# A sandwich block on one core: the repeated part and the last five blocks of a hand-ordered kernel in a new order

## The chip, the cores and the metric

The kernel runs on one core of a Trainium2 chip. The metric is the device time of one execution in microseconds (us); the runs of a kernel are given by their median. A profile is one more execution, recorded with the start and the length of every instruction; its span runs from the first instruction to the last.

PE is the matmul engine, DVE, ACT and POOL are the three engines for elementwise work, SP issues the transfers (DMA). Each engine works off its own list in order; between engines, semaphores hold an instruction until what it needs is there.

## What is computed

Four batches of 2048 rows of 256 numbers. Per batch, an attention step and a feed-forward step, each of them between two norms and added to its input:

```python
x = x + layernorm(attn(layernorm(x)))
x = x + layernorm(ffn(layernorm(x)))

def attn(x):
    q, k, v = split(x @ weight_qkv, 3)        # parts of the contraction in fp16
    s = softmax((q / sqrt(256)) @ k.T)
    return (s @ v) @ out_w.T + out_b

def ffn(x):
    x_prev = x shifted by one row, zeros in front
    r = sigmoid((mu_r * x + (1 - mu_r) * x_prev) @ W_r.T)
    k = (mu_k * x + (1 - mu_k) * x_prev) @ W_k.T
    return r * (square(relu(k)) @ W_v.T)
```

## The kernel before

**Blocks.** The rows are cut into 32 blocks of 256 (eight to a batch). A block is a tile of 128 partitions x 2 halves x 256 numbers. The query and key weights are folded into one matrix G, the value and output weights into w_o. Numbers for a matmul are split into a high and a low fp16 tile (`H` and `L` in a name), and a product is then two or three fp16 matmuls.

**The order is written out.** `HEAD`, `LOOP` and `TAIL` are strings of words; `run` calls the function of each word in turn, and every engine's list is the order in which its words stand. `HEAD` prepares weights and the first blocks, `LOOP` is run for block numbers 3 to 26, `TAIL` holds what is left of the last blocks. In `LOOP`, `sM@0` is the current block and `yy@-5` the block five before; in `TAIL`, `@T1` is the last block (31), `@T5` is block 27. What follows a slash chooses a half, or an engine for each half.

**The words that matter here**, by stage:

- Attention. `aS`, `aP`, `aN`, `aM`, `aD`: statistics, power (POOL), norm and split of the input, for a block nine later. `tM` (PE), `tH` (ACT), `tL` (DVE): the block's queries times G. `sM@g/i/h` (PE, 20 matmuls for two): scores of rows half i against half h of the keys, in a buffer of PSUM; there are two such buffers. `sX` (DVE): their maximum; `sB` (DVE): both maxima made into the bias; `sE` (ACT): exponential, which reads the buffer for the last time; `sH` (ACT) and `sL` (DVE): split; `sT` (SP): transpose by DMA into the tile PT. `pv` (PE, 80 matmuls): PT times values, z. `zH`, `zL`: split of z; `pj` (PE): times w_o; `dn` and `y` (DVE): division by the softmax sum, bias.
- Norms after it. `bS` (DVE) statistics, `bP` (POOL) power, `bN` norm, `bA` add to x; the same with c for the second norm, into `hN` and `hF`. Or, in the last blocks: sums on the way of `y` (`q`), `bM` mean (POOL), `bQ` squares (ACT), `bR` power (POOL). The last block has `bY` and `bX` (DVE): subtract the mean, then scale and add in one step.
- Feed-forward. `hX`, `hT`, `hO`: the normed rows transposed by DMA; `hV`, `hW` by PE and a copy instead in the last three blocks; `hC`, `hD` the difference to the row before; `mk`, `mr` the two mixes (DVE; `mA` and `mB` on ACT and POOL instead); `kH`, `kL`, `rH`, `rL` their splits; `kM`, `kR`, `kA` (PE, ACT, DVE): square of relu; `uH`, `uL` its split; `rM`, `rT` (PE, ACT): the gate; `oM` (PE) and `yy` (DVE): its product. Then the same norm forms with d (`dS`, `dP`, `dN`, `dA`; `dM`, `dQ`, `dR`; `dY`, `dX`), and `st` (SP) the store. `ld` loads a block of x again.
- Of the last block alone: `zC` (ACT, L741) copies z unsplit, and `pf`, `kf`, `rf`, `of` are projections in fp32 with weights put together by `wR`.

In the profile most matmuls stand under L173 (a helper) and those of `pv` under L442; the maximum is L396, the exponential L409, the first split L416 and L422, the norms L271 (ACT) and L273 (DVE and POOL), power L213 and L237, squares L227, an add of d L723, `dX` and `bX` L247, `hQ` L542.

Of the kernel before, what the change touches and what calls it, by code (L numbers as in the profile page):

```python
# [64 lines left out]
yy@T10 zH@T7 tM@T4 tH@T4 tL@T4 sM@T5/0/1 sM@T5/0/0 zL@T7 pj@T7 kM@T9 tM@T3 dn@T7 hF@T8/act/pool
sX@T5/0/1 sX@T5/0/0 hN@T8/pool/pool sB@T5/0 y@T7 dS@T10 dn@T6 hX@T8/pool sE@T5/0/0 sE@T5/0/1
sH@T5/0/1 sM@T5/1/0 sX@T5/1/0 sH@T5/0/0 sL@T5/0/0 hT@T8 tH@T3 sM@T5/1/1 hC@T8 sL@T5/0/1 sX@T5/1/1
pv@T6/0/8 sB@T5/1 sM@T4/0/0 sT@T5/0/0 hO@T8/pool hD@T8/dve tL@T3 bS@T7 rM@T9 sE@T5/1/0 kR@T9
sM@T4/0/1 bP@T7 sE@T5/1/1 mr@T8 sH@T5/1/0 sX@T4/0/0 bN@T7/act/pool kA@T9 uH@T9/dve sT@T5/0/1
pv@T6/8/16 sL@T5/1/0 sM@T4/1/1 sH@T5/1/1 mk@T8 sX@T4/0/1 rT@T9 sB@T4/0 sL@T5/1/1 rH@T8/dve bA@T7/dve  # L70
sE@T4/0/1 uL@T9/dve cS@T7 zH@T6 kH@T8/dve sM@T4/1/0 cP@T7 sT@T5/1/1 dP@T10 kL@T8/pool zL@T6
sE@T4/0/0 sX@T4/1/1 sH@T4/0/1 sX@T4/1/0 pj@T6 hC@T7 y@T6 sL@T4/0/1 kM@T8 sB@T4/1 bS@T6
dN@T10/act/pool sT@T5/1/0 kR@T8 sH@T4/0/0 kA@T8 oM@T9 hF@T7/pool/pool hN@T7/act/act bP@T6 sT@T4/0/1
hX@T7/pool yy@T9 pv@T5/0/8 dS@T9 sE@T4/1/1 sM@T3/0/1 hT@T7 hO@T7/pool bN@T6/dve/act sE@T4/1/0
rL@T8/dve bA@T6/dve tM@T2 sH@T4/1/1 sL@T4/0/0 hD@T7/pool tH@T2 cS@T6 sX@T3/0/1 tL@T2 mk@T7 sH@T4/1/0
sL@T4/1/1 kH@T7/act sM@T3/0/0 pv@T5/8/16 cP@T6 hF@T6/act/dve hN@T6/act/act rM@T8 sT@T4/0/0 kL@T7/dve
hX@T6/pool sX@T3/0/0 hC@T6 wR/w_v/dve dn@T5 zH@T5 uH@T8/act sB@T3/0 zL@T5 hT@T6 uL@T8/dve sT@T4/1/1
kM@T7 pj@T5 rT@T8 sE@T3/0/0 dP@T9 sL@T4/1/0 mr@T7 y@T5 hO@T6/dve sE@T3/0/1 bS@T5 dN@T9/dve/pool
rH@T7/dve sM@T3/1/0 kR@T7 hC@T5 dA@T10/dve ld@T5 rL@T7/dve hD@T6/pool oM@T8 sT@T4/1/0 sM@T3/1/1
sX@T3/1/0 bP@T5 pv@T4/0/8 pv@T4/8/16 bN@T5/act/act sH@T3/0/0 wR/w_k/pool sM@T2/0/1 sX@T3/1/1  # L80
bA@T5/pool sL@T3/0/0 sH@T3/0/1 cS@T5 sT@T3/0/0 yy@T8 sB@T3/1 mk@T6 kA@T7 cP@T5 sM@T2/0/0 sE@T3/1/1
sL@T3/0/1 rM@T7 uH@T7/act sH@T3/1/1 sE@T3/1/0 zH@T4 uL@T7/dve sL@T3/1/1 sH@T3/1/0 hN@T5/dve/pool
hF@T5/act/act sT@T3/0/1 mr@T6 dS@T8 hX@T5/pool sX@T2/0/1 kH@T6/act zL@T4 sX@T2/0/0 st@T10 rT@T7
dP@T8 kL@T6/pool oM@T7 kM@T6 sM@T2/1/0 sB@T2/0 dA@T9/dve hT@T5 sE@T2/0/1 sL@T3/1/0 yy@T7 sE@T2/0/0
rH@T6/act dn@T4 sH@T2/0/1 hO@T5/dve rL@T6/pool dS@T7 sH@T2/0/0 pj@T4 y@T4 hD@T5/pool sM@T2/1/1 ld@T4
st@T9 sT@T3/1/1 dP@T7 tM@T1 sL@T2/0/1 kR@T6 bS@T4 mr@T5 sT@T3/1/0 pv@T3/0/8 tH@T1 bP@T4 sX@T2/1/1
sX@T2/1/0 kA@T6 sB@T2/1 pv@T3/8/16 sL@T2/0/0 tL@T1 dN@T7/act/pool bN@T4/pool/act sE@T2/1/0
dA@T7/pool sH@T2/1/0 sM@T1/0/0 mk@T5 kH@T5/pool bA@T4/dve cS@T4 dn@T3 sE@T2/1/1 sT@T2/0/0 sM@T1/0/1
kL@T5/pool sT@T2/0/1 rM@T6 cP@T4 kM@T5 zH@T3 hN@T4/act/dve sH@T2/1/1 zL@T3 sL@T2/1/0 hF@T4/act/act
ld@T1 sL@T2/1/1 rT@T6 sX@T1/0/0 sX@T1/0/1 hX@T4/pool rH@T5/pool sB@T1/0 uH@T6/pool sE@T1/0/1  # L90
sT@T2/1/0 pj@T3 kR@T5 sH@T1/0/1 uL@T6/pool rL@T5/pool sE@T1/0/0 dN@T8/act/pool y@T3/01/q sM@T1/1/1
bM@T3 hT@T4 hC@T4 wR/w_o/dve oM@T6 kA@T5 sM@T1/1/0 sT@T2/1/1 st@T7 dn@T2 sH@T1/0/0 sX@T1/1/1 yy@T6
rM@T5 hO@T4/pool bQ@T3 hD@T4/dve bR@T3 pv@T2/0/8 ld@T3 sL@T1/0/0 mk@T4 sX@T1/1/0 sB@T1/1
bN@T3/act/pool pv@T2/8/16 sT@T1/0/0 kH@T4/pool dA@T8/dve bA@T3/dve sE@T1/1/0 sL@T1/0/1 sT@T1/0/1
# [877 lines left out]
```

## Time and profile before

| what | us |
|---|---|
| median of three runs | 799.85 (798.22 to 801.39) |
| the profiled execution | 798.83 |
| its span | 797.0 |
| PE busy in the span | 781.7 |
| PE busy in 100 to 200, 200 to 300, 300 to 400 | 99.71, 100.00, 100.00 |
| PE busy in 720 to 740, 740 to 760 | 20.00, 19.93 |
| DVE busy in 650 to 700, 720 to 740, 740 to 760 | 47.58, 17.85, 19.66 |
| ACT and POOL busy in 650 to 700 | 29.01, 20.34 |

The granted clock of PE was 0.997 over the span. A line of a timeline gives start, length, engine, line, operation, what is written and read, the shape, and in brackets how long the engine had been idle and which instruction ended that. A block of the repeated part takes 23.7 us. The first matmul of the last five blocks' part starts at 638.86, the last of `pv` ends at 768.52.

### The profile page before, as it was taken

The page shows a single profiled execution, that of the slowest core. Times are in us where ns is not written, and L with a number is a line of the kernel's source. Part 1 is how long each engine was busy: PE and PEld are TensorE (multiplying, and loading weights), DVE is VectorE, ACT ScalarE, POOL GpSimd, SP SyncE. Part 2 cuts the span into 40 slices and gives each one's busy share as a digit, 9 for nine tenths or more (in the row PEclk, how much of TensorE's full clock was granted, in tenths as well). Part 3 has the DMA queues.
Part 4 walks back from the last instruction along what each step waited for, and adds up shares of the span by engine and source line. Part 5 has one row for each costly group of instructions (what it writes and reads, how often), then busy time and mean ns, then how long its engine had stood idle before and what let it go on. Part 6 is the DMA issues. An engine that isn't in the chain of part 4 may idle for free.

```text
span 797.0 us, 15916 instructions
## 1 busy us (share of the span) xinstructions
PE 781.7 (98%) x5803; PEld 574.3 (72%) x5803; DVE 696.9 (87%) x1606; ACT 536.3 (67%) x889; POOL 464.6 (58%) x632
## 2 busy tenths in 40 slices
...
GB/s 238 178 146 172 148 153 145 139 133 143 155 141 134 154 119 143 155 157 119 168 117 140 145 169 124 139 118 128 143 123 120 119 119 61 139 122 130 144 71 66
DMA packets 351199, 109.18 MB, mean 137 GB/s; under 512 B 324624, under 2 KB 351120, under 8 KB 351120
## 3 DMA queue, kind: packets, MB, share of 16 engines
...
q14 instruction: 34, 0.28, 0.1%
q10 hardware_dynamic: 272, 0.26, 0.1%
...
## 4 chain that ended last, share of the span: by engine, by line
PE 90%; DVE 5%; DMA 1%; ACT 1%; issue 1%; POOL 0%; POOLq 0%; SPq 0%; ACTq 0%; DVEq 0%
PE z L442 33%; PE s L173 33%; DMA PT__995<-hl__1240 1%; DMA xa__110<-in_x_dram 1%; PE warm__211 L806 0%; PE op__11019 L173 0%; PE warm__520 L806 0%; PE k__11262 L173 0%; DVE x__10522 L247 0%; DVE sm L818 0%; PE o__11191 L173 0%; PE op__10541 L173 0%; DVE mxmx__10570 L396 0%; DVE pstsA__150 L254 0%; PE r__10479 L173 0%
## 5 line engine op out<-in xcount | busy, mean ns | idle before, releaser
L173 PEld LDWEIGHTS <-w_kH 128*128 128x128 f16 x248 | 24.3, 98 | 8.2 <-issue 0.5
L173 PEld LDWEIGHTS <-GH 128*128 128x128 f16 x192 | 18.8, 98 | 3.7 <-DVE tL__334 L372 0.7
L442 PEld LDWEIGHTS <-X__271 128*128 128x128 f16 x160 | 15.7, 98 | 2.2
L442 PEld LDWEIGHTS <-X__6669 128*128 128x128 f16 x160 | 15.7, 98 | 2.2
L442 PEld LDWEIGHTS <-X__5273 128*128 128x128 f16 x160 | 15.6, 98 | 2.2
L442 PEld LDWEIGHTS <-X__189 128*128 128x128 f16 x160 | 15.5, 98 | 2.3 <-issue 0.5
L442 PEld LDWEIGHTS <-X__233 128*128 128x128 f16 x160 | 15.7, 98 | 1.8
L442 PEld LDWEIGHTS <-X__718 128*128 128x128 f16 x160 | 15.7, 98 | 1.8
L442 PEld LDWEIGHTS <-X__324 128*128 128x128 f16 x160 | 15.7, 98 | 1.8
L442 PEld LDWEIGHTS <-X__4575 128*128 128x128 f16 x160 | 15.7, 98 | 1.8
L442 PEld LDWEIGHTS <-X__571 128*128 128x128 f16 x160 | 15.7, 98 | 1.8
L442 PEld LDWEIGHTS <-X__1783 128*128 128x128 f16 x160 | 15.7, 98 | 1.8
L442 PEld LDWEIGHTS <-X__3179 128*128 128x128 f16 x160 | 15.7, 98 | 1.8
L442 PEld LDWEIGHTS <-X__7367 128*128 128x128 f16 x160 | 15.7, 98 | 1.8
L442 PEld LDWEIGHTS <-X__3877 128*128 128x128 f16 x160 | 15.7, 98 | 1.8
L442 PEld LDWEIGHTS <-X__1141 128*128 128x128 f16 x160 | 15.7, 98 | 1.8
L442 PEld LDWEIGHTS <-X__2481 128*128 128x128 f16 x160 | 15.7, 98 | 1.8
L442 PEld LDWEIGHTS <-X__5971 128*128 128x128 f16 x160 | 15.6, 98 | 1.8
L173 PEld LDWEIGHTS <-GL 128*128 128x128 f16 x128 | 12.5, 98 | 3.4 <-issue 0.9
L173 PEld LDWEIGHTS <-w_kL 128*128 128x128 f16 x124 | 12.1, 98 | 1.4
L329 POOL TENSOR_TENSOR X__718<-xa__485,X__718 128x256 f16<-128x256 f32 x1 | 1.7, 1657 | 16.4 <-ACT xa__485 L271 16.4
L273 POOL TENSOR_SCALAR xa__344<-xa__344,rsrna__455,nmrna__456 128x128 f32<-128x128 f32 x2 | 0.9, 449 | 17.2 <-ACT X__571 L271 17.2
...
## 6 DMA issues: line engine op xcount, KB each, us to landing
...
```

The source lines that it names most:

```text
L173: nc.tensor.matmul(out_ap, l, r, start=(i == 0), stop=(i == len(pairs) - 1))
L273: eng(e).tensor_scalar(dst, src, rs[:, j:j + 1], nm[:, j:j + 1], ALU.mult, ALU.add)
L329: eng(e).tensor_tensor(Xh[:, :, 2, :], T["xa", g][:, :, P:D], Xh[:, :, 1, :], ALU.subtract)
L442: nc.tensor.matmul(z[:, int(c), 0:QB], a, p, start=(kt == 0 and n == 0), stop=(kt == KT - 1 and n == len(prs) - 1))
```

## The change

`LOOP` and `TAIL` are new strings; all words do what they did. `HEAD` stays. One function (`aL`) gets an argument for halves that no word uses.

In `LOOP` the same words stand in another order, but for `aN@9`, which moves from POOL to DVE. On PE the two first score halves change places and `sM@0/1/0` stands ahead of `tM@1`; on DVE `tL@1` stands ahead of `sX@0/1/0` and `sX@0/1/1`; on POOL `bA@-2` stands ahead of `aM@9`.

In `TAIL` the order is new on every engine, and some fifty elementwise steps are on another engine (norms, splits, differences, adds). Three things change in form: `zC@T1` and the second part of `pv@T1` are cut in two by the halves of z; block 30's last norm uses statistics on DVE (`yy@T2`, `dS@T2`, `dP@T2`) in place of sums, squares on ACT and `dR`; and in the last block the half j=1 goes first after `of`.

The diff, with `LOOP` whole and of `TAIL` the rows that the prediction speaks of:

```diff
 LOOP = """
-sM@0/0/0 yy@-5 sM@0/0/1 aS@9 zH@-2 dS@-5 hF@-3/act/act zL@-2 dP@-5 sX@0/0/1 kM@-4 pj@-2 dn@-2
-pv@-1/0/8 sX@0/0/0 sB@0/0 hN@-3/act/act y@-2 tM@1 aP@9 sM@0/1/0 dN@-5/act/act sM@0/1/1 aN@9/pool
-hX@-3/pool kR@-4 dA@-5/pool aT@8 bS@-2 hC@-3 kA@-4 sE@0/0/0 sE@0/0/1 bP@-2 sH@0/0/0 sH@0/0/1 hT@-3
-sL@0/0/0 bN@-2/act/act rM@-4 hO@-3/dve sL@0/0/1 tH@1 aL@11 pv@-1/8/16 hD@-3/pool ld@0 sT@0/0/1
-aM@9/pool uH@-4 sX@0/1/0 sX@0/1/1 rT@-4 bA@-2/pool sB@0/1 sE@0/1/0 mk@-3 kH@-3 sH@0/1/0 cS@-2
-uL@-4/pool sE@0/1/1 oM@-4 sH@0/1/1 tL@1 sL@0/1/0 sT@0/0/0 mr@-3 sL@0/1/1 st@-5 kL@-3/pool sT@0/1/0
-rH@-3 rL@-3/pool sT@0/1/1 aD@9/pool cP@-2
+sM@0/0/1 sM@0/0/0 yy@-5 aS@9 zH@-2 hF@-3/act/act dS@-5 zL@-2 dP@-5 sX@0/0/1 kM@-4 pj@-2 dn@-2
+pv@-1/0/8 sX@0/0/0 sM@0/1/0 hN@-3/act/act sB@0/0 y@-2 tM@1 aP@9 dN@-5/act/act sM@0/1/1 aN@9/dve
+hX@-3/pool kR@-4 sE@0/0/0 aT@8 bS@-2 hC@-3 kA@-4 dA@-5/pool sE@0/0/1 bP@-2 sH@0/0/0 sH@0/0/1 hT@-3
+sL@0/0/0 rM@-4 hO@-3/dve sL@0/0/1 bN@-2/act/act tH@1 aL@11 pv@-1/8/16 tL@1 hD@-3/pool ld@0 sT@0/0/1
+uH@-4 sX@0/1/0 sX@0/1/1 rT@-4 bA@-2/pool sB@0/1 sE@0/1/0 mk@-3 kH@-3 sH@0/1/0 cS@-2 aM@9/pool
+uL@-4/pool sE@0/1/1 oM@-4 sH@0/1/1 sL@0/1/0 sT@0/0/0 mr@-3 sL@0/1/1 st@-5 kL@-3/pool sT@0/1/0 rH@-3
+rL@-3/pool sT@0/1/1 aD@9/pool cP@-2
 """
 TAIL = """
...
-bQ@T2 mB@T3/r/pool mA@T3/k kR@T4 kA@T4 bR@T2 bN@T2/act/pool bA@T2/dve rH@T3/act dQ@T5 cS@T2
-sT@T1/1/1 dN@T6/dve/pool mB@T3/k/pool kH@T3/dve uH@T4/pool pv@T1/8/16 uL@T4/dve cP@T2 rL@T3/dve
-zC@T1 dR@T5 hN@T2/act/act pf@T1/1 dn@T1 dA@T6/dve pf@T1/0 y@T1/0 hV@T2 y@T1/1 hC@T2 bS@T1/0/q
-dN@T5/act/pool bS@T1/1/q kL@T3/pool hW@T2/act hD@T2/pool rM@T4 rT@T4 st@T6 bY@T1/0 mA@T2/r mk@T2
-bP@T1/0/q kH@T2/act bX@T1/0 bP@T1/1/q oM@T4 kM@T3 bY@T1/1 rM@T3 hC@T1 kL@T2/pool yy@T4/01/q dM@T4
-kM@T2 kR@T3 dQ@T4 cS@T1/0/q bX@T1/1 kA@T3 cS@T1/1/q cP@T1/0/q uH@T3/act hQ@T1/0 rT@T3 mB@T2/r/pool
-cP@T1/1/q hV@T1/0 uL@T3/dve hQ@T1/1 kR@T2 hV@T1/1 dA@T5/dve rH@T2/act hW@T1/act oM@T3 kA@T2
-rL@T2/dve dR@T4 uH@T2/act dN@T4/act/act yy@T3/01/q hD@T1/pool uL@T2/dve mk@T1 dA@T4/dve rM@T2 st@T5
-oM@T2 rT@T2 dM@T3 mr@T1 kf@T1 yy@T2/01/q rf@T1 dQ@T3 dM@T2 dR@T3 st@T4 kR@T1 dQ@T2 kA@T1 of@T1/1
-rT@T1 of@T1/0 dN@T3/dve/dve dR@T2 dA@T3/dve yy@T1/0 yy@T1/1 dS@T1/0/q dN@T2/pool/act dY@T1/0
-dS@T1/1/q st@T3 dA@T2/pool dP@T1/0/q st@T2 dX@T1/0 st@T1/0 dY@T1/1 dP@T1/1/q dX@T1/1 st@T1/1
...
+sE@T5/1/1 hD@T8/dve sE@T5/1/0 cS@T7 cP@T7 mr@T8 pv@T6/8/16 hC@T7 sH@T5/1/0 sM@T4/1/1 sX@T4/0/0
+sL@T5/1/0 tL@T3 sX@T4/0/1 uL@T9/pool dn@T5 sT@T5/0/1 sH@T5/1/1 sB@T4/0 sE@T4/0/0 sL@T5/1/1 sE@T4/0/1
+mk@T8 rH@T8/dve sX@T4/1/1 zH@T6 hN@T7/act/act sT@T5/1/0 rM@T9 sM@T4/1/0 oM@T9 sH@T4/0/1 zL@T6 rT@T9
...
+sM@T3/1/1 kR@T7 sL@T3/0/0 sX@T3/1/1 bP@T5 wR/w_o/dve hX@T6/pool kA@T7 oM@T8 bN@T5/pool/act sX@T3/1/0
+sB@T3/1 sL@T3/0/1 sT@T4/0/1 bA@T5/pool sT@T4/0/0 sE@T3/1/0 pv@T4/0/8 sM@T2/0/0 dA@T9/dve uH@T7/act
...
+hO@T6/pool hD@T6/dve zH@T4 oM@T7 zL@T4 mk@T6 hX@T5/dve pj@T4 hT@T5 sX@T2/0/1 sL@T3/1/1 sT@T3/1/0
+sB@T2/0 kH@T6/pool tM@T1 rT@T7 sM@T2/1/0 yy@T7 mr@T6 hC@T5 dP@T8 y@T4 sE@T2/0/0 tH@T1 kL@T6/pool
+rH@T6/pool wR/w_r/pool sT@T3/1/1 dS@T7 rL@T6/pool bS@T4 hO@T5/dve hD@T5/dve sE@T2/0/1 sM@T2/1/1
...
+sH@T2/1/1 hT@T4 sX@T1/0/0 rM@T6 kA@T6 sX@T1/0/1 kH@T5/act y@T3/01/q sB@T1/0 kL@T5/pool sL@T2/1/1
+sE@T1/0/0 rL@T5/pool hO@T4/dve kM@T5 sT@T2/1/0 rT@T6 sT@T2/0/1 uH@T6/dve hD@T4/pool sM@T1/1/1
...
+sL@T1/0/1 bQ@T3 mk@T4 bR@T3 dA@T8/dve bN@T3/act/act kH@T4/pool st@T7 st@T8 sX@T1/1/0 ld@T2 sB@T1/1
+bA@T3/pool yy@T6 kR@T5 sT@T1/0/0 cS@T3 kL@T4/pool kA@T5 sE@T1/1/0 dS@T6 sH@T1/1/0 cP@T3 uH@T5/act
...
+sT@T1/0/1 pv@T1/0/8 mA@T3/r kA@T4 kH@T3/dve bR@T2 sT@T1/1/1 bN@T2/act/act uH@T4/dve mB@T3/r/pool
+kL@T3/dve pv@T1/8/16/0 pv@T1/8/16/1 bA@T2/dve zC@T1/0 cS@T2 zC@T1/1 dN@T6/dve/dve pf@T1/1 hC@T2
+rH@T3/dve cP@T2 dA@T6/dve pf@T1/0 uL@T4/dve hN@T2/dve/pool y@T1/0 y@T1/1 rL@T3/pool bS@T1/0/q hV@T2
+bS@T1/1/q bY@T1/1 hW@T2/act hD@T2/pool bP@T1/0/q rM@T4 kM@T3 rT@T4 oM@T4 mA@T2/r dR@T5 bY@T1/0 mk@T2
+bX@T1/0 mB@T2/r/pool kR@T3 bP@T1/1/q kA@T3 dN@T5/act/act st@T6 kH@T2/act rH@T2/act cS@T1/0/q
+yy@T4/01/q hC@T1 cP@T1/0/q dM@T4 bX@T1/1 kL@T2/dve uH@T3/act cS@T1/1/q rM@T3 dQ@T4 rT@T3 uL@T3/pool
+kM@T2 kR@T2 hQ@T1/0 cP@T1/1/q hV@T1/0 dA@T5/dve hQ@T1/1 hV@T1/1 rL@T2/dve st@T5 kA@T2 oM@T3
+hW@T1/act uH@T2/act yy@T3/01/q dR@T4 rM@T2 hD@T1/pool uL@T2/dve oM@T2 mk@T1 kf@T1 dN@T4/act/act
+dA@T4/dve dM@T3 rT@T2 mr@T1 dQ@T3 dR@T3 kR@T1 yy@T2 dS@T2 kA@T1 rf@T1 dN@T3/pool/act dA@T3/dve rT@T1
+of@T1/1 dP@T2 st@T3 of@T1/0 st@T4 dN@T2/pool/act yy@T1/1 dS@T1/1/q yy@T1/0 dY@T1/1 dA@T2/pool st@T2
+dP@T1/1/q dS@T1/0/q dX@T1/1 st@T1/1 dY@T1/0 dP@T1/0/q dX@T1/0 st@T1/0
 """
...
     @op
-    def aL(g, q="sync"):
-        eng(q).dma_start(out=blk("xa", g), in_=rows(x, g))
+    def aL(g, q="sync", js="01"):
+        eng(q).dma_start(out=blk("xa", g)[:, cut(js), :], in_=rows(x, g)[:, cut(js), :])
 
```

More of the change, by code (lines that the diff above doesn't have):

```diff
@@ L64 @@
 TAIL = """
[L65 to L94, printed above, removed]
@@ L95 @@
-sH@T1/1/0 st@T8 rT@T5 uH@T5/act cS@T3 sE@T1/1/1 dS@T6 cP@T3 mr@T4 dP@T6 hC@T3 kL@T4/pool sL@T1/1/0
-hN@T3/act/act hV@T3 sT@T1/1/0 uL@T5/dve rH@T4/act wR/w_r/pool sH@T1/1/1 oM@T5 hW@T3/dve ld@T2 zH@T2
-zL@T2 yy@T5/01/q sL@T1/1/1 rL@T4/dve dM@T5 pj@T2 hD@T3/pool kM@T4 mA@T3/r y@T2/01/q bM@T2 pv@T1/0/8
-bQ@T2 mB@T3/r/pool mA@T3/k kR@T4 kA@T4 bR@T2 bN@T2/act/pool bA@T2/dve rH@T3/act dQ@T5 cS@T2
-sT@T1/1/1 dN@T6/dve/pool mB@T3/k/pool kH@T3/dve uH@T4/pool pv@T1/8/16 uL@T4/dve cP@T2 rL@T3/dve
-zC@T1 dR@T5 hN@T2/act/act pf@T1/1 dn@T1 dA@T6/dve pf@T1/0 y@T1/0 hV@T2 y@T1/1 hC@T2 bS@T1/0/q
@@ L107 @@
-rT@T1 of@T1/0 dN@T3/dve/dve dR@T2 dA@T3/dve yy@T1/0 yy@T1/1 dS@T1/0/q dN@T2/pool/act dY@T1/0
-dS@T1/1/q st@T3 dA@T2/pool dP@T1/0/q st@T2 dX@T1/0 st@T1/0 dY@T1/1 dP@T1/1/q dX@T1/1 st@T1/1
+yy@T10 tM@T4 zH@T7 sM@T5/0/0 hC@T8 zL@T7 hN@T8/pool/pool tH@T4 dn@T7 sM@T5/0/1 hF@T8/dve/pool tL@T4
+hX@T8/pool pj@T7 kM@T9 sX@T5/0/0 sX@T5/0/1 sB@T5/0 sE@T5/0/0 y@T7 hT@T8 sE@T5/0/1 tM@T3 sH@T5/0/0
+dS@T10 kR@T9 hO@T8/pool sM@T5/1/0 bS@T7 dn@T6 sM@T5/1/1 pv@T6/0/8 kA@T9 sX@T5/1/0 sL@T5/0/0 bP@T7
+bN@T7/pool/pool tH@T3 sM@T4/0/0 sH@T5/0/1 bA@T7/pool sM@T4/0/1 sX@T5/1/1 sB@T5/1 sL@T5/0/1 uH@T9/act
@@ new lines @@
+sE@T5/1/1 hD@T8/dve sE@T5/1/0 cS@T7 cP@T7 mr@T8 pv@T6/8/16 hC@T7 sH@T5/1/0 sM@T4/1/1 sX@T4/0/0
+sL@T5/1/0 tL@T3 sX@T4/0/1 uL@T9/pool dn@T5 sT@T5/0/1 sH@T5/1/1 sB@T4/0 sE@T4/0/0 sL@T5/1/1 sE@T4/0/1
+mk@T8 rH@T8/dve sX@T4/1/1 zH@T6 hN@T7/act/act sT@T5/1/0 rM@T9 sM@T4/1/0 oM@T9 sH@T4/0/1 zL@T6 rT@T9
+hF@T7/pool/act sT@T5/0/0 sL@T4/0/1 sX@T4/1/0 hX@T7/pool pj@T6 sB@T4/1 tM@T2 pv@T5/0/8 ld@T5 yy@T9
+kH@T8/pool hT@T7 sE@T4/1/0 kL@T8/pool sH@T4/1/0 sE@T4/1/1 hO@T7/dve kM@T8 sT@T5/1/1 y@T6 rL@T8/pool
+sM@T3/0/0 dS@T9 hD@T7/pool mr@T7 sL@T4/1/0 mk@T7 tH@T2 bS@T6 dP@T10 sM@T3/0/1 wR/w_v/dve pv@T5/8/16
@@ new lines @@
+dP@T9 kH@T7/dve sH@T4/1/1 rM@T8 sL@T4/1/1 bP@T6 bN@T6/pool/act kL@T7/pool dN@T10/act/dve sM@T3/1/0
+sX@T3/0/0 dA@T10/pool sX@T3/0/1 sH@T4/0/0 kR@T8 kA@T8 bA@T6/pool sB@T3/0 sE@T3/0/0 tL@T2 sT@T4/1/0
+dN@T9/dve/pool sH@T3/0/0 cS@T6 sL@T4/0/0 rH@T7/act uH@T8/act zH@T5 dn@T4 zL@T5 uL@T8/dve pj@T5 kM@T7
+sE@T3/0/1 rT@T8 cP@T6 hN@T6/act/pool y@T5 wR/w_k/pool sT@T4/1/1 bS@T5 sH@T3/0/1 hF@T6/pool/pool
+sM@T3/1/1 kR@T7 sL@T3/0/0 sX@T3/1/1 bP@T5 wR/w_o/dve hX@T6/pool kA@T7 oM@T8 bN@T5/pool/act sX@T3/1/0
@@ new lines @@
+sB@T3/1 sL@T3/0/1 sT@T4/0/1 bA@T5/pool sT@T4/0/0 sE@T3/1/0 pv@T4/0/8 sM@T2/0/0 dA@T9/dve uH@T7/act
+hT@T6 sT@T3/0/0 sE@T3/1/1 yy@T8 pv@T4/8/16 sM@T2/0/1 sT@T3/0/1 st@T10 cS@T5 uL@T7/pool rL@T7/dve
+sH@T3/1/0 cP@T5 hN@T5/pool/act rM@T7 ld@T4 sX@T2/0/0 hF@T5/act/act sH@T3/1/1 hC@T6 sL@T3/1/0 dS@T8
+hO@T6/pool hD@T6/dve zH@T4 oM@T7 zL@T4 mk@T6 hX@T5/dve pj@T4 hT@T5 sX@T2/0/1 sL@T3/1/1 sT@T3/1/0
+sB@T2/0 kH@T6/pool tM@T1 rT@T7 sM@T2/1/0 yy@T7 mr@T6 hC@T5 dP@T8 y@T4 sE@T2/0/0 tH@T1 kL@T6/pool
+rH@T6/pool wR/w_r/pool sT@T3/1/1 dS@T7 rL@T6/pool bS@T4 hO@T5/dve hD@T5/dve sE@T2/0/1 sM@T2/1/1
@@ new lines @@
+sH@T2/0/0 bP@T4 sX@T2/1/1 dP@T7 bN@T4/pool/act sL@T2/0/0 sX@T2/1/0 st@T9 hC@T4 dN@T8/dve/act
+bA@T4/pool ld@T3 sB@T2/1 dN@T7/pool/pool kM@T6 cS@T4 sE@T2/1/0 cP@T4 mr@T5 tL@T1 sH@T2/1/0
+hF@T4/dve/pool sH@T2/0/1 sL@T2/1/0 sE@T2/1/1 sL@T2/0/1 pv@T3/0/8 mk@T5 hN@T4/dve/act pv@T3/8/16
+zH@T3 hX@T4/pool rH@T5/act dn@T3 sM@T1/0/0 kR@T6 sM@T1/0/1 zL@T3 dA@T7/pool sT@T2/0/0 pj@T3
+sH@T2/1/1 hT@T4 sX@T1/0/0 rM@T6 kA@T6 sX@T1/0/1 kH@T5/act y@T3/01/q sB@T1/0 kL@T5/pool sL@T2/1/1
+sE@T1/0/0 rL@T5/pool hO@T4/dve kM@T5 sT@T2/1/0 rT@T6 sT@T2/0/1 uH@T6/dve hD@T4/pool sM@T1/1/1
```

4 lines of the change are left out of this document (added).

## The prediction

> **What bounds the kernel now.** I read the busy shares first, then a table of stretches, then who waited for whom, then the chain that ended last, and last the timelines of one block of the repeated part and of the last 60 us.
>
> ```profile
> PE 781.7 (98%) x5803; PEld 574.3 (72%) x5803; DVE 696.9 (87%) x1606; ACT 536.3 (67%) x889; POOL 464.6 (58%) x632
> ...
> 400.00:500.00 100.00, 100.00 (x747) 72.79 (x745) 87.53 (x205) 68.77 (x113) 65.51 (x87) 1.00 0.67 142
> ...
> 760.00:780.00 20.00, 18.15 (x153) 15.52 (x152) 15.29 (x49) 13.68 (x32) 18.08 (x29) 1.00 0.17 41
> 780.00:797.00 17.00, 9.59 (x62) 7.83 (x61) 12.34 (x33) 7.52 (x18) 9.42 (x15) 0.87 0.23 78
> ```
>
> PE (second column of the stretches) has no gap from 100 to 740 us: nothing taken off DVE, ACT or POOL there can shorten the run, it can only start a gap. What is left to win is the drain: 9.3 us of idle PE after 760. The waits of PE from 640 us on are few:
>
> ```profile
> PE op__11019 L173 <- ACT zf__11009 L741: 0.7, 1, 0.7
> PE r__11113 L173 <- DVE y__11129 L681: 0.5, 1, 0.5
> PE ht__11177 L578 <- DVE h__11171 L542: 0.4, 1, 0.4
> PE k__11136 L173 <- DVE ka__11149 L655: 0.3, 1, 0.3
> ```
>
> and the chain ends like this (start, us, what):
>
> ```profile
> 786.78 0.60 ACT junkd__11290 L227 x2
> 787.40 0.61 ACT junkd__11290 L227 x2
> ...
> 789.75 0.07 issue
> 789.82 0.20 POOL nmrnd__11304 L238
> ...
> 790.79 1.26 POOL x__10826 L723
> 792.05 0.56 POOL rsrnd__11326 L213
> ...
> 793.84 0.48 DVE x__10522 L247
> ```
>
> The end is set not by the last block's own matmuls (the last is issued by 789.7) but by POOL, busy with block 30's norm: squares on ACT, power, add, and only then block 31's power.
>
> **The repeated part: 0.** Three moves. Two first norms (aN) go from POOL to DVE, a first score half (sM 1/0) passes tM on PE, tL passes the two reductions on DVE. These rows hold the cover:
>
> ```profile
> 67.80 0.73 DVE L273 TENSOR_SCALAR X__571<-xa__489,rsrna__682,nmrna__683 128x256 f16<-128x256 f32 x2
> ...
> 508.04 1.23 DVE L422 SCALAR_TENSOR_TENSOR hl__7395<-p__7387,hl__7395 128x1024 f16<-128x1024 f32 x1 [0.97 <-ACT hl__7395 L416]
> ...
> 513.42 1.22 DVE L396 TENSOR_REDUCE mxmx__7342<-s 128x1 f32<-128x1024 f32 x1 [0.93 <-PE s L173]
> ...
> 506.87 0.20 ACT L409 ACTIVATION_READ_ACCUMULATOR p__7389<-s,bb__7319,esc 128x1 f32 x1
> ...
> 509.83 0.58 ACT L365 ACTIVATE tH__7419<-tps__7327 128x512 f16<-128x512 f32 x1
> ...
> 514.74 0.69 ACT L671 ACTIVATE th__7473<-r__7404,sc 128x512 f32<-128x512 f32 x1 [3.81 <-PE r__7404 L173]
> ```
>
> aN costs DVE 0.73 (the first row, same shape). It stands before bS, kA and sL; sL at 508.04 had 0.97 of idle before it, for ACT, so it starts when it did. bS ends at 507.1 and not 506.4; bP and the ACT norm behind it ran at 508.85, after sH, so that hides too. sM 1/0 now starts 1.09 earlier (tM's length), at 507.81, and needs the buffer of the first exponential, free at 505.8: even the second is done at 507.07. tM ends 2.16 later, 511.2; ACT does tH then and not at 509.83, inside the 3.81 it idled before th. tL then runs 511.9 to 512.5 on DVE, ahead of the reductions; the second of these starts at 513.6 instead of 513.42, its scalar is there at 515.0, and ACT is busy with th until 515.32 anyway. Without this cover 0.2 a block would be lost, 20 to 24 times (4 to 5 us). POOL loses 1.09 a block. SP's order in the block stays. Bounds -0.2 to +0.5; I take 0.
>
> **The last five blocks up to the last value product: -0.2.** PE's list is the same set of matmuls; those up to the end of pv of block 31 add up to 129.2 us (10 of 0.109 per tM, 20 of 0.216 per two sM, 80 of 0.109 per pv, 12 of 0.109 per projection). Before, they took from 638.86 to 768.52, 129.66: so 0.46 is to be had at most. Elementwise work moves: 53 words change engine. By the rows' durations DVE's list falls from 134.1 to 132.9 us, ACT's from 89.5 to 85.3, POOL's grows from 75.7 to 83.7. DVE idled 10.4 us between 639 and 768, so it has reserve, but it isn't spread evenly. I went through the score halves: sM needs a buffer that an exponential frees (reduction 1.14, scalar 0.27, exponential 1.3 with its accumulator). Most have over 0.5 us. Four are tight in the new order: block 28's third half is wanted at 665.35, its buffer free at 665.25; block 30's first wanted at 702.98, free at 702.75 (wR of 0.65 and kA of 0.60 now stand between the two reductions of block 29); block 30's fourth 718.84 against 718.65 (tH of block 31 goes first on ACT); block 31's third 739.29 against 739.30. Before, the last was already 0.02 late. SP's queue: transposes land 3.6 to 5.7 after issue; the latest, of block 31's last scores, issues at 758.8 against 759.37 before, wanted at 763.7. The load of block 30 and the first transpose of block 31 now stand behind the store of block 24, which waits for an add on DVE at 746.5; that transpose is wanted at 759.3. So 0 to 0.3 is lost of the 0.46: -0.2, bounds -0.46 and +1.0 (three of the four missed by one scalar-sized step of 0.3).
>
> POOL is slowed by DVE and DVE by POOL in the trace: the same POOL difference took 1.04 or 1.45, and a DVE add of two numbers a row that takes 0.15 took 0.95 at 741.43 beside a POOL add. Such stretched DVE rows add up to some 2.3 us in these blocks; 11% more POOL work makes +0.25, which is in the bound. The Trainium skill, page SBUF — State Buffer, section Who interferes with whom, is harder on this change: POOL and a DVE instruction with two SBUF inputs exclude each other for a whole instruction. Taken literally for all 8.0 us moved to POOL, DVE would lose up to 8.0 us and the run would end near 805.7; the rows above say a small part of that.
>
> **Last z and last chain by halves: -2.0.** (a) zC: 0.65 lay between the last matmul (768.52) and pf (769.17). The first half is now copied while PE does the 24 matmuls (2.6 us) of the second; a half should take 0.37 (0.60 for 512 elements, 1.06 for 1024 in another ACT row), beside pf's matmuls on the first half (0.43). -0.65, or -0.2 if the halves are not tracked apart. (b) Given back: +0.5. From y to the second hQ DVE has y 0.79, bS 1.44, bY 0.52, mk 0.79, bX 0.39, kA 0.60, cS 0.72, yy 0.69, bX 0.39, kL 0.60, cS 0.72, hQ 0.33, dA 0.60, hQ 0.33 = 8.91; before 8.31 and 0.28 of waits, ending 779.80. From 771.21 - 0.85 that ends 779.3. On POOL the second half's power now stands behind dR (1.3, up to 2.3) and mB (1.18): 772.2 + 0.6 + 1.3 + 1.18 + 0.6 = 775.9 against 776.3 when DVE wants it; a slow power makes it late by up to 0.6. I take 779.6, then PE 0.22 + 1.31 and yy of block 29 at 781.3 instead of 781.64. (c) From there DVE: yy 0.69, uL 0.60, mk 0.79, dA 0.60, mr 0.79, yy 0.60, dS 1.25, kA 0.60, ending 787.25. dS takes the place of ACT's squares and is new in front of kA; kA waited until 786.92 and of was issued at 787.81, now about 787.3. (d) of makes the half j=1 first; yy now takes that half first, at 788.35 instead of 789.80. Behind it yy 0.35, dS 0.72, yy 0.35, dY 0.26, dS 0.72, dX 0.39, dY 0.26, dX 0.39 = 3.44, so 791.8 against 794.32. POOL: power of block 30 from 786.65 (0.9), half norm 0.53, ACT's half by 788.5, add 1.26 to 789.8, then 31's power (0.6, 0.73), ready for dX at 790.75. With 0.1 to 0.2 for slow powers: 792.1. The store after it is the same.
>
> Sum against the profiled execution: 0 - 0.2 - 0.65 + 0.5 - 1.85 = -2.2, span 797.0 to 794.8. That execution took 798.83 in all and the median of three is 799.85 (798.22 to 801.39), so the forecast is 799.85 - 2.2 = 797.65. I call 0.5% (4.0 us) what a measurement of this kernel can tell from no change.
>
> **Rivals.** (1) The drain gains little: the waits are not split by halves, or POOL's powers take 1.28 and 1.59 as two rows show, and the second half starts over 1 us late. (a) gives -0.2, (d) loses its 0.95, so about -0.8: 799.0. For: POOL's list grows. Against: the built program gives pf's two matmuls and the two yy separate waits. (2) Slower: one mechanism, the score buffers. If DVE is one entry later at the tight hand-offs, PE stands for the reduction and the exponential that then run alone, 1.14 + 1.3 = 2.4. Two misses cancel the gain (+2.6), three give +5.0: 804.9, over 0.5%. For: four slacks of 0.25 or less. Against: they follow fixed steps behind PE itself, so a late PE moves both sides. (3) More: no give-back and no tail stall, -0.46 - 0.65 - 2.4 = -3.5, and 0.5 from faster powers: 795.8.
>
> **Numbers.** Forecast 0.52, rival 1 0.22, rival 2 0.18, rival 3 0.08. All but half of rival 2's worst and some of 3 lie within 4.0 us: same 0.78, slower 0.16, faster 0.06. The range for 8 in 10 goes from rival 3's edge, 795.6, over rival 1 to one miss beyond no change, 802.2.
>
> **What would show it.** After: PE busy 100 of 100 in 400 to 500; last z ending near 768.3; pf right behind it with no wait on zf; no squares of block 30 on ACT; the last dX ending near 792. Wrong if PE waits for exponentials (L409) between 650 and 745, if a gap recurs in every block, or if POOL still releases the last dX after 793.

## The result, and the profile after

The changed kernel takes 804.62 us (median of six runs, 804.26 to 806.76) against 799.39 for the kernel before (six runs, 798.22 to 801.39): a ratio of 1.0075, 95% interval 1.0064 to 1.0085. That is 5.2 us slower by the medians and 6.0 by the ratio. The forecast was 797.7 and the range ended at 802.2. The profiled execution took 804.48, its span is 802.4 (797.0 before), and the granted clock 0.998 (0.997 before). So 5.4 us have to be found in the span.

The busy times of the changed kernel, for the whole span and then by stretch (start and end, length, PE, PEld, DVE, ACT, POOL, clock, DMA share, GB/s):

```profile
PE 786.2 (98%) x5803; PEld 574.4 (72%) x5803; DVE 746.6 (93%) x1646; ACT 538.2 (67%) x880; POOL 457.8 (57%) x599
...
400.00:500.00 100.00, 99.42 (x750) 72.90 (x749) 97.47 (x209) 70.79 (x113) 59.75 (x78) 1.00 0.66 143
760.00:780.00 20.00, 19.43 (x169) 16.90 (x168) 15.61 (x46) 9.36 (x24) 13.36 (x17) 1.00 0.52 94
780.00:802.00 22.00, 13.73 (x91) 10.43 (x88) 16.88 (x49) 11.17 (x24) 14.47 (x24) 0.93 0.18 60
```

The second line is the one that matters. PE has lost its 100 of 100 in the middle of the run, and DVE has gone from 87.5 to 97.5. The 50 us more of DVE in the whole span are far more than the 20 norms of 0.73 each that were moved to it (14.6). The small scale of `dn` (L479), which is done once a block, gives the length of a block: it starts at 147.3 and 507.6, 15 blocks apart, so 24.02 us a block; before, at 147.2 and 502.7, 23.70. From block 23 on, where no `aN` is left, a block of PE's work takes 23.7 again. By then 4.4 us are lost: the first matmul of the last blocks, a `tM`, starts at 643.07; in the profile of before it starts at 638.70 (by the trace, not at 638.86).

Three DVE instructions of a block of the kernel before, each with the POOL instruction that will stand beside it after the change (start, length, engine, line, what):

```profile
502.69 0.23 DVE L479 TENSOR_SCALAR ds__7272<-ds__7272,two 128x2 f32<-128x2 f32 x1
503.93 1.16 POOL L558 TENSOR_TENSOR hh__7237<-h__7321,hh__7237 128x512 f16<-128x512 f32 x1
...
513.95 1.16 POOL L276 TENSOR_TENSOR Lup__7469<-ka__7371,Hup__7468 128x512 f16<-128x512 f32 x1
514.88 0.91 DVE L600 SCALAR_TENSOR_TENSOR mk__7480<-dd__7461,mus,hT__7384 128x256 f32<-128x256 f32 x2
...
516.70 0.23 DVE L204 TENSOR_SCALAR vesc__7490<-mvsc__7489,sc 128x2 f32<-128x2 f32 x1
517.19 1.15 POOL L276 TENSOR_TENSOR Lkp__7484<-mk__7480,Hkp__7483 128x512 f16<-128x512 f32 x1 [2.09 <-ACT Hkp__7483 L164]
```

And the same ones in a block of the changed kernel, in order of time:

```profile
507.58 1.22 DVE L479 TENSOR_SCALAR ds__7272<-ds__7272,two 128x2 f32<-128x2 f32 x1
507.61 1.16 POOL L558 TENSOR_TENSOR hh__7228<-h__7331,hh__7228 128x512 f16<-128x512 f32 x1
...
511.13 0.73 DVE L273 TENSOR_SCALAR X__7367<-xa__6723,rsrna__7350,nmrna__7351 128x256 f16<-128x256 f32 x2
...
513.92 1.23 DVE L422 SCALAR_TENSOR_TENSOR hl__7395<-p__7373,hl__7395 128x1024 f16<-128x1024 f32 x1 [0.32 <-ACT hl__7395 L416]
...
519.83 1.15 POOL L276 TENSOR_TENSOR Lup__7469<-ka__7371,Hup__7468 128x512 f16<-128x512 f32 x1
519.97 1.69 DVE L600 SCALAR_TENSOR_TENSOR mk__7480<-dd__7463,mus,hT__7385 128x256 f32<-128x256 f32 x2
...
522.39 1.16 POOL L276 TENSOR_TENSOR Lkp__7484<-mk__7480,Hkp__7483 128x512 f16<-128x512 f32 x1 [1.41 <-ACT Hkp__7483 L164]
522.58 0.99 DVE L204 TENSOR_SCALAR vesc__7490<-mvsc__7489,sc 128x2 f32<-128x2 f32 x1
```

`aN` costs what was forecast, and the idle time of `sL` goes from 0.97 to 0.32 as forecast. But three DVE instructions that the change never touched are longer: the scale 1.22 in place of 0.23, `mk` 1.69 in place of 0.91, the scale in `cS` 0.99 in place of 0.23. Each stands beside a POOL instruction that reads two tiles. The two scales end when that one has ended (508.80 beside 508.77; 523.57 beside 523.55), and so in 19 of the 20 blocks, 0.02 to 0.07 after it; `mk`, which is two instructions, ends 0.68 after `uL`. From start to next start they cost 0.99, 0.79 and 0.77 more, with `aN`'s 0.64 some 3.2 a block. Other instructions cost 0.4 less, since an instruction that follows another without a wait starts some 0.08 before that one's recorded end. So DVE needs 2.8 more, and it had 2.8 of idle time before (0.97, 0.93, 0.52, 0.26, 0.16). Of this 0.3 can't be had: the idle before `sL` is a wait for ACT's `hl`, and ACT by then waits for DVE's bias itself. That is the 0.3 by which the block is longer.

PE loses it at one place in a block, the first matmul of `pj` that reads `zL` (L467, DVE). In the kernel before DVE ends that split 0.9 ahead of PE. In the changed kernel this lead is 0.74, 0.43 and 0.12 in three blocks from 121 on, and from 193 on PE stands in each of 15 blocks until the split is there:

```profile
505.66 0.69 DVE L467 SCALAR_TENSOR_TENSOR Lzp__7226<-z,Hzp__7225 128x512 f16<-128x512 f32 x1
506.40 0.10 PEld L173 LDWEIGHTS <-Lzp__7226 128*128 128x128 f16 x1 [0.42 <-DVE Lzp__7226 L467]
```

The matmul starts 0.36 to 0.45 after the one ahead of it, and before 0.11. Only about half of that shows as idle PE, since a matmul's record lasts 0.27; so the 99.42 of 100 tell less than was lost.

Who PE waited for from 640 on, and the end of the chain that ended last:

```profile
PE k__11166 L173 <- DVE Lkp__11116 L276: 0.9, 1, 0.9
PE ht__11184 L578 <- DVE h__11181 L542: 0.5, 1, 0.5
PE op__11009 L173 <- ACT zf__10995 L741: 0.5, 1, 0.5
PE r__11147 L173 <- DVE ka__11108 L655: 0.4, 1, 0.4
```

```profile
780.42 1.13 POOL mr__11094 L621
781.56 0.52 POOL rsrnb__11050 L213
782.08 0.03 issue
782.10 0.54 DVE x__10808 L247
...
793.52 2.01 PE o__11300 L173 x8
...
795.61 0.43 DVE y__11313 L685
...
797.04 0.56 POOL rsrnd__11325 L213
...
799.20 0.48 DVE x__10808 L247
```

The wait for `zf` is still there, 0.5 in place of 0.7; a wait of 0.9 for a split behind the second `bX` is new; and the first `yy` after `of` starts when all of `of` is done (793.52 + 2.01), not after its half. From the last `pv` to the end of the span it is 29.0 us (773.4 to 802.4); before, 28.5 (768.5 to 797.0). The drain, which was to win 2.0, has lost 0.5. So the 5.4 us of the span are 4.4 in the repeated part, 0.55 from the first matmul of the last blocks to the last `pv` (130.3 in place of 129.8), and 0.45 behind it.

### The profile page after: what moved, and what is told of

Its sections match the earlier page's. It is cut to its first block, busy times and chain, and to the rows that moved or that the text cites. A ratio compares the mean times of both kernels' runs of the same rounds, so it can differ in the third digit from the quotient of the medians.

```text
span 802.4 us, 15881 instructions
## 1 busy us (share of the span) xinstructions
PE 786.2 (98%) x5803; PEld 574.4 (72%) x5803; DVE 746.6 (93%) x1646; ACT 538.2 (67%) x880; POOL 457.8 (57%) x599
## 4 chain that ended last, share of the span: by engine, by line
DVE 45%; PE 37%; issue 10%; ACT 5%; DMA 1%; POOL 1%; POOLq 0%; DVEq 0%; SPq 0%; ACTq 0%
PE z L442 14%; PE s L173 13%; DMA PT__10474<-hl__10802 1%; DMA xa__110<-in_x_dram 1%; DVE mxmx__9316 L396 0%; DVE mxmx__1735 L396 0%; DVE mxmx__7319 L396 0%; DVE mxmx__6272 L396 0%; DVE mxmx__4178 L396 0%; DVE mxmx__3480 L396 0%; DVE mxmx__2084 L396 0%; DVE mxmx__6970 L396 0%; DVE mxmx__5923 L396 0%; DVE mxmx__5574 L396 0%; DVE mxmx__5225 L396 0%
```

## The experiments

Ratios are against the kernel before in the same session (its medians there: 798.7 to 798.8), with 4 to 11 executions of each kernel.

**Which part.** First the repeated part and the last blocks, one at a time: `LOOP` of the change with `TAIL` of before, and the reverse.

> The changed repeated part with the last five blocks of before. My theory (the loss is in the repeated part: DVE gets the two norms, 0.64 a block, and three of its instructions are held by POOL for 0.8 to 1.0 each, so DVE fills the block and a block takes 24.0 in place of 23.7): the last five blocks' part starts near 643.2 in place of 638.9, DVE busy 97 of 100 in 400 to 500, time about +4.4 over before (+4.0 to +4.9). Rival (the loss is in the last blocks, score-buffer hand-offs, as the prediction's second rival had it): within 0.5 of before.

803.28 us, ratio 1.0057 (1.0045 to 1.0070). A block is 24.02 long, DVE 97.42 in 400 to 500, the last blocks' part starts at 643.7 (638.7 before), the span is 802.1.

> The repeated part of before with the changed last five blocks. My theory: they lose 0.6 up to the last value product and 0.5 behind it, about +1.0 over before (+0.3 to +1.5). The prediction's own view of the last blocks: -2.2. Its rival of missed score buffers: +2.6 to +5.0.

799.41 us, ratio 1.0011 (1.0003 to 1.0020). Its span is 797.4. So of the 0.75% some 0.57 come from the repeated part and 0.11 from the last blocks; by the spans, 5.1 and 0.4 of 5.4 us. In `new_tail` the last blocks lose 0.2 up to the last `pv` and 0.45 behind it. No exponential is among what PE waits for in them: the rival of the missed score buffers, at its price of 2.6 to 5.0, falls.

**Order or engine.** Then the two things that the change does to the repeated part, one at a time.

```diff
 (loop_aN_pool: LOOP of the change)
-... sM@0/1/1 aN@9/dve
+... sM@0/1/1 aN@9/pool
 (only_aN_dve: LOOP of before)
-... sM@0/1/1 aN@9/pool
+... sM@0/1/1 aN@9/dve
```

> The changed order of the repeated part, but the norm aN on POOL as before; last blocks of before. My theory (aN's place decides: on DVE it adds 0.64, and off POOL it lets hX start just as DVE comes to its small scale by two, which then takes 1.22 in place of 0.23): that scale takes 0.23 again, DVE has idle time in each block, PE busy 99.9 of 100 in 400 to 500, time within 0.6 of before. Rival (the new order itself costs, with bA ahead of aM on POOL against mk and cS): +2.5 to +4.4.

798.69 us, ratio 0.9998 (0.9989 to 1.0007), the scale 0.23, PE 100 of 100 in 400 to 500. The new order alone costs nothing and wins nothing, as forecast.

> The kernel before, with aN in the repeated part on DVE and nothing else changed. My theory: DVE gains 0.64 and 1.0 (the small scale beside hX), 1.6 a block against 2.9 of idle time; not all of that can be used, so 0 to +2.0, less than the changed repeated part loses. Rival (aN alone is the whole of it, the order nothing): +4.4.

808.13 us, ratio 1.0120 (1.0106 to 1.0133): +9.3. My expectation was far too low, since it priced the scale alone. A block takes 24.3 (the scale starts at 463.6 and 487.9), and its timeline shows the other two as well, `mk` worse than in the change:

```profile
487.92 1.22 DVE L479 TENSOR_SCALAR ds__6923<-ds__6923,two 128x2 f32<-128x2 f32 x1
...
499.71 2.08 DVE L600 SCALAR_TENSOR_TENSOR mk__7133<-dd__7114,mus,hT__7035 128x256 f32<-128x256 f32 x2
500.18 1.33 POOL L276 TENSOR_TENSOR Lup__7122<-ka__7021,Hup__7121 128x512 f16<-128x512 f32 x1
...
502.71 1.00 DVE L204 TENSOR_SCALAR vesc__7143<-mvsc__7142,sc 128x2 f32<-128x2 f32 x1
```

So with `aN` on DVE the new order loses half of what the old one does. PE's place of waiting is the same: the lead of `zL` is 0.27 at 122 and gone from 146 on, and from 170 on the matmul behind it starts 0.68 to 0.70 after the one ahead of it.

**Load or meeting.** If DVE's load were the cause, only less work on it would help. If it is the meetings with POOL, a move that takes no work off DVE must bring the time back. Three tests: `dn` one place earlier on DVE; `uL` ahead of `bA` and `aM` on POOL; and the opposite, `aN` on DVE in addition, with POOL's list as it was (the norm is then computed twice, with the same values).

```diff
 (dn_early: LOOP of the change)
-... sX@0/0/1 kM@-4 pj@-2 dn@-2
+... dn@-2 sX@0/0/1 kM@-4 pj@-2
 (uL_early: LOOP of the change)
-uH@-4 sX@0/1/0 sX@0/1/1 ... aM@9/pool uL@-4/pool
+uH@-4 uL@-4/pool sX@0/1/0 sX@0/1/1 ... aM@9/pool
 (aN_twice: LOOP of before)
-... aN@9/pool hX@-3/pool
+... aN@9/pool aN@9/dve hX@-3/pool
```

> The changed repeated part with aN on DVE and last blocks of before, as in new_loop (803.3), but dn stands one place earlier on DVE, ahead of the first maximum. The same DVE work. My theory (POOL's hX holds the small scale by two for 1.0, and a block is over its 23.7 by only 0.3): the scale takes 0.23 to 0.5, a block is 23.7 long again, time within 0.7 of before (-4 against new_loop). Rival (DVE is full by its amount of work and the order of waits, the long scale being only where a wait shows): still +3 to +4.5 over before.

798.44 us, ratio 0.9995 (0.9986 to 1.0004). One block, and the stretch 400 to 500:

```profile
490.15 1.15 POOL L276 TENSOR_TENSOR Lup__7122<-ka__7021,Hup__7121 128x512 f16<-128x512 f32 x1
491.27 0.87 DVE L600 SCALAR_TENSOR_TENSOR mk__7133<-dd__7116,mus,hT__7036 128x256 f32<-128x256 f32 x2
493.06 0.23 DVE L204 TENSOR_SCALAR vesc__7143<-mvsc__7142,sc 128x2 f32<-128x2 f32 x1
...
501.45 0.23 DVE L479 TENSOR_SCALAR ds__7245<-ds__7245,two 128x2 f32<-128x2 f32 x1
...
502.62 1.16 POOL L558 TENSOR_TENSOR hh__7228<-h__7331,hh__7228 128x512 f16<-128x512 f32 x1
```

```profile
400.00:500.00 100.00, 100.00 (x746) 72.79 (x744) 89.38 (x213) 69.13 (x113) 61.16 (x79) 1.00 0.65 142
```

The same DVE instructions, one of them one place earlier, and 8 of 100 of DVE's busy time are gone. The scale now runs 1.2 ahead of `hX`; and `mk` and `cS` are short again without having been moved, because DVE is no longer late: it stands idle 0.90 ahead of `tL`, and so comes to `mk` when POOL's `uL` ends, and to `cS` before its `kL`. The split `zL` is ready 0.91 ahead of PE, as before.

> As new_loop, but on POOL uL stands ahead of bA and aM, so that mk on DVE meets aM and not uL. My theory: mk falls from 1.69 to about 1.1, which is more than the 0.3 a block that DVE lacks; a block of 23.7, time within 0.7 of before. Rival (mk's length is the DVE's own): +4.4 as new_loop.

798.45 us, ratio 0.9994 (0.9985 to 1.0002). `mk` takes 0.87 (not 1.1, as I expected: `aM`, beside which it now stands, doesn't hold it, and is longer itself, 1.42 in place of 0.87) and `cS`'s scale 0.23, while the scale of `dn` is still 1.22. DVE is busy 93.05 of 100, and that fits. To remove one meeting is enough; the one after it went with it.

> The kernel before, with aN in the repeated part done on POOL as before and then once more on DVE at its changed place (the same values are written twice). DVE gets 0.64 a block more, POOL's list stays as it was. My theory (what costs 9 in only_aN_dve is that POOL, free of aN, meets three DVE instructions): DVE's idle time takes the 0.64, the small scale stays 0.23, time within 0.7 of before. Rival (0.64 more on DVE is itself too much): +5 to +9.

798.66 us, ratio 0.9998 (0.9989 to 1.0007). PE 100 of 100. DVE's additional norm does no harm, though it takes 1.55 where it now stands, beside POOL's `dA`. But the theory saw less than there was, for `mk` (1.9) and `cS`'s scale (1.0) are long here too, and DVE is busy 98.62 of 100. By busy share times length of a block DVE does 23.4 us in this kernel and in the change; here it just fits into 23.7, since DVE never waits 0.3 before `sL`: from 169 on `zL` is ready 0.06 to 0.09 ahead of its matmul, where it was 0.9, and PE stands for it at most 0.02.

The last test of this kind: the order of before, where `aN` on DVE cost 9.3, with `dn` one place earlier.

```diff
 (aN_dve_dn_early: LOOP of before)
-... sX@0/0/1 kM@-4 pj@-2 dn@-2 ... aN@9/pool
+... dn@-2 sX@0/0/1 kM@-4 pj@-2 ... aN@9/dve
```

> The repeated part in its order of before, with aN on DVE as in only_aN_dve (+9.3 over before), and dn one place earlier on DVE; last blocks of before. My theory (the 9.3 come from the small scale behind hX, and what follows when DVE's idle time is gone): scale 0.23, a block 23.7, time within 0.7 of before. Rival (the old order has no room for aN on DVE, the new one was needed): +2 to +9.

798.27 us, ratio 0.9997 (0.9988 to 1.0005), a block of 23.7. One word's place gives back all of the 9.3 us. `mk` (1.39) and `cS`'s scale (1.18) are still long here, and DVE is busy 94.35 of 100: with the scale of `dn` short there is room for them.

**The last blocks.** In `new_tail`, whose repeated part is that of before, the milestones can be laid beside those of the kernel before; only its last blocks start 0.25 earlier (638.45 against 638.70), with the same repeated part. This is its timeline at the last z, at the second `bX` and at the end:

```profile
768.47 0.66 ACT L741 ACTIVATE zf__10995<-z 128x256 f32<-128x256 f32 x2 [2.63 <-PE z L442]
...
772.23 1.04 POOL L595 TENSOR_TENSOR dd__11048<-hT__11012 128x512 f32<-128x512 f32 x1 [0.17 <-ACT hT__11012 L164]
773.23 0.63 POOL L213 TENSOR_TENSOR rsrnb__11050<-vesb__11034,nhalf 128x1 f32<-128x1 f32 x1
...
776.56 0.56 POOL L213 TENSOR_TENSOR rsrnb__11050<-vesb__11034,nhalf 128x1 f32<-128x1 f32 x1
777.15 0.53 DVE L247 SCALAR_TENSOR_TENSOR x__10808<-y__11028,rsrnb__11050,x__10808 128x256 f32<-128x256 f32 x1
...
788.57 1.99 PE L173 MATMUL o__11300<-W32w_v__9762,ka__11276 128*128 128x256 f32 x8
790.66 0.42 DVE L685 SCALAR_TENSOR_TENSOR y__11313<-th__11298,o__11300 128x256 f32<-128x256 f32 x1 [1.55 <-PE o__11300 L173]
```

Both halves of `zf` are copied together after the last matmul, though the first half of z was done some 2.6 earlier; and the first `yy` waits for both halves of `of`. In the program the first of each pair carries the wait, on the last matmul of both halves, and the second carries none: the two halves lie in one PSUM tile, and the waits are made by tile. So I gave the halves tiles of their own. The diff shows where the tiles are made; the matmuls, the copy and `yy` name them accordingly.

```diff
 def of(g, js="01"):
-    tok32("o", T["ka", g], "w_v", g, js)
+    if js == "1":
+        T["o1", g] = ps_z.tile([P, 2, 512], F32, tag="z", ...)[:, :, 0:QB]
+    tok32("o1" if js == "1" else "o", T["ka", g], "w_v", g, js)
 def pv(g, k0, k1, cs="01"):
+    if g == NG - 1 and ("z1", g) not in T:
+        T["z1", g] = ps_s.tile([P, 2, 512], F32, tag="s", ...)
```

> As new_tail (+0.6 over before), but the two halves of the last z, and of the last block's last product o, lie in separate PSUM tiles, so that each half has a wait of its own. My theory (in the change both halves wait for the last matmul of both, since the waits are by tile): the first half of z is copied 2 us earlier and pf starts 0.2 earlier; the first yy starts about 1.0 earlier behind of, and the end comes 1.0 to 1.5 earlier: -0.6 to -0.9 against before. Rival (POOL's powers set the end in any case): within 0.4 of new_tail.

798.57 us, ratio 1.0000 (0.9992 to 1.0009); span 796.8 against 797.4 of `new_tail`. The waits part as expected:

```profile
765.85 0.38 ACT L744 ACTIVATE zf__10996<-z 128x256 f32<-128x256 f32 x1
768.27 2.20 PE L173 MATMUL op__11010<-W32w_o__9970,zf__10996 128*128 128x256 f32 x8
768.47 0.38 ACT L744 ACTIVATE zf__10996<-zs__10894 128x256 f32<-128x256 f32 x1 [2.24 <-PE zs__10894 L444]
...
777.37 0.53 DVE L247 SCALAR_TENSOR_TENSOR x__10808<-y__11029,rsrnb__11051,x__10808 128x256 f32<-128x256 f32 x1 [0.35 <-POOL rsrnb__11051 L213]
...
788.78 1.13 PE L173 MATMUL oz__11301<-W32w_v__9762,ka__11277 128*128 128x256 f32 x4
...
790.01 0.42 DVE L688 SCALAR_TENSOR_TENSOR y__11315<-th__11299,oz__11301 128x256 f32<-128x256 f32 x1 [0.68 <-ACT y__11279 L271]
```

`pf` starts 0.64 earlier, and all of it is lost again by the second `bX`, which waits for POOL, 0.35 of idle DVE (777.37; it was 777.15). `yy` starts 1.23 behind `of` in place of 2.09, and the last `dX` ends at 794.08 in place of 794.73. Half of my expectation: what is won ahead of POOL isn't kept. So I took the second power out from behind `dR` and `mB`; the splits `kH` and `rH` also go ahead of `dN@T5` on ACT.

```diff
-... bP@T1/0/q ... mA@T2/r dR@T5 bY@T1/0 mk@T2 bX@T1/0 mB@T2/r/pool kR@T3 bP@T1/1/q
+... bP@T1/0/q bP@T1/1/q ... mA@T2/r bY@T1/0 mk@T2 bX@T1/0 mB@T2/r/pool dR@T5 kR@T3
-... uL@T3/pool kM@T2 kR@T2 hQ@T1/0 cP@T1/1/q hV@T1/0 dA@T5/dve hQ@T1/1 hV@T1/1
+... kM@T2 kR@T2 hQ@T1/0 cP@T1/1/q hV@T1/0 uL@T3/dve hQ@T1/1 hV@T1/1 dA@T5/dve
```

> As true_halves (-0.1), with the second half's power of the last block put ahead of mB and dR on POOL (mB ahead of dR), and around it the two splits kH and rH ahead of the norm dN of block 27 on ACT, uL of block 29 on DVE, and the add dA of block 27 behind the second hQ. My theory (POOL sets this stretch: the second bX waits until 777.4 for a power that stands behind 2.9 of dR and mB): bX 0.4 earlier, the second hQ ends 0.5 to 0.9 earlier, of as well, time -0.5 to -1.0 against before. Rival (DVE's list alone sets it, as the prediction had it): within 0.3 of true_halves.

798.72 us, ratio 1.0005 (0.9996 to 1.0014). A miss; the rival's value, within 0.3 of `true_halves`, is what came. The second `bX` starts at 777.10 without a wait, and the second `hQ` ends at 780.23 (780.78 in `true_halves`); but `of` is not earlier, 788.85 against 788.78. PE has a new wait:

```profile
PE o__11239 L173 <- DVE Lup__11210 L276: 0.3, 1, 0.3
```

Of the 0.55, that `uL` gets 0.29 (it starts at 783.02, and at 783.31 in `true_halves`); it takes 1.07 here, beside POOL's `hD`, and took 0.69 there. So it ends no earlier: what was left of the gain went into another meeting of the two engines.

**Both together.** Last, the changed kernel with only `dn` moved, and with everything mended.

> The changed kernel as it is, with dn one place earlier on DVE in the repeated part. My theory (the loss of the change is the repeated part's, and the last blocks add 0.3 to 1.0 whatever they follow): as new_tail, +0.3 to +1.0 over before. Rival (the two parts hurt each other where they meet): +2 and more.

799.91 us, ratio 1.0017 (1.0007 to 1.0027): +1.2 by the medians, a little over what I expected, and well under the rival. One word takes the change from 1.0075 to 1.0017. The two parts do hurt each other a little: from the first matmul of the last blocks to the last `pv` it takes 130.38 here, and 129.99 in `new_tail`.

> The changed kernel with all that was mended: dn early in its repeated part, true halves and the second power first in its last blocks. My theory: as power_first, -0.5 to -1.0 against before. Rival (DVE, fuller in the changed repeated part, carries a lag into the last blocks): +0.5 and more over power_first.

798.54 us, ratio 1.0001 (0.9992 to 1.0009). The -0.5 to -1.0 did not come, and the rival's +0.5 did not either. In its profile the drain is 0.55 shorter than before (28.0 against 28.55), and the way to the last `pv` 0.55 longer (130.35 against 129.8): nothing is won. None of the versions beats the kernel before by more than its measurement can tell.

## Why the prediction was wrong

**The repeated part: forecast 0, bounds -0.2 to +0.5; it was +4.5 by the times and +5.1 by the span of `new_loop`.** This is the step that failed, and within it one sentence: "POOL loses 1.09 a block". I took that for relief. It meant that what stood behind `aN` on POOL, `hX`, started at once, beside the scale of `dn`. `aN`'s 0.64 and this 1.0 made DVE later by 1.6; that took the 1.2 of idle time (0.26 and 0.93) ahead of the maxima, and this idle time had kept `mk` behind POOL's `uL` and `cS` clear of `kL`. With these two, 3.2 a block came on DVE where the prediction had 0.73, and the lead of 0.9 that `zL` had over PE was gone. What was said of the order move by move (score halves, `tM`, `tL`) was right: with `aN` on POOL it costs 0. That `aN` is covered before `sL` was right too: `aN_twice`. "Without this cover 0.2 a block would be lost, 20 to 24 times (4 to 5 us)" met the size by chance; it named another cause, and I gave it no chance.

**The weighing of the rule.** I set the Trainium skill (SBUF — State Buffer, section Who interferes with whom: POOL and a DVE instruction with two SBUF inputs hold each other for a whole instruction) against one row (a DVE add of 0.15 that took 0.95), allowed 0.25 for it, and looked for it in the last blocks alone. That row, and the repeated part's rows now, go with the page: in 19 of the 20 blocks the scale is held until POOL's instruction has ended. `mk` reads two tiles; the scale reads one and a factor from another, and no run here tells by which of the page's conditions it is held. What the rule would have asked for is to lay the two engines' lists side by side by start times after the move, in the part that runs 20 times.

**The last blocks up to the last `pv`: forecast -0.2; +0.2.** From their first matmul it took 130.0 in `new_tail` (638.45 to 768.45) and 129.8 before (638.70 to 768.52). That is within the bounds and wrong in sign; the last `pv` ends 0.07 earlier only because the repeated part, the same in both, ended 0.25 earlier in that execution. In the change it took 130.3. There PE stands 0.2 at each of two score halves that start just when the exponential of their buffer has ended (661.08 after 661.03, 670.04 after 669.99), and 0.26 for the last transpose (768.87). So the tight hand-offs of rival 2 are there, at 0.2 each and not at 2.4.

**(a) the copy of z: forecast -0.65; -0.2**, from y starting 0.27 earlier less the 0.07 above. The lower value stood in the text, for the case that the halves aren't tracked apart, and that is the case. The price of a half was right: 0.38 a copy, and with tiles of its own y starts at 770.51, 0.70 earlier than before.

**(b) the give-back: forecast +0.5; +1.0.** The second `hQ` ended at 780.56, not 779.6: 9.62 after the start of `y`, where the forecast had 9.24 and the kernel before 8.59. POOL's term was mis-summed: I started its first power at 772.2 and left out `hD` (1.04), which stands ahead of it; it started at 773.23, and the second ended at 777.1, not 775.9. But DVE itself came to the second `bX` only then and stood idle 0.05, less than the 0.3 that the forecast had put in for a late power. What is over the forecast lies in DVE's own rows, the largest in the first `hQ`: 0.64 beside POOL's `uL`, and 0.41 before. Removing the wait won nothing in the end (`power_first`).

**(c) and (d), the last chain: forecast -1.85 in all; -0.35** (from the end of the second `hQ` to that of the last `dX`, 14.17 in `new_tail` and 14.52 before). `of` was to be issued near 787.3 and came at 788.57; the first `yy` was to start at 788.35, by its half, and came at 790.66, by the whole tile: 2.09 behind `of`. The last `dX` ended at 794.73, not 792.1. What was said against rival 1, that the built program gives the two `yy` separate waits, was misread: the first has the wait for both. That POOL would no longer release block 30's norm last was right: between 789.94 and 791.21 it adds, and the next power waits for DVE.

So the drain went the way of rival 1, and further, since (b) was twice its price and the last chain gave 0.35 where that rival left 0.9: it lost 0.5 (28.95 from the last `pv` to the end of `new_tail`'s span, 28.5 before) where it was to win 2.0. Rival 2's time (804.9) lay near the result by luck: its cause, missed score buffers, makes about 0.4 of the loss and not 7. "A gap recurs in every block" was the sign named for a wrong forecast, and it is what happened.
